# Counting neighbours with 32-column products, four in one PSUM bank, two tiles at a time

## The chip, the core and the metric

The kernel runs on one core of a Trainium2 chip. The metric is the device time in microseconds (us) of one launch; less is better.

## What is computed

Four layers of a graph network over N = 3327 nodes with D = 64 features share one dense-stored, sparse adjacency matrix `adj`. Each layer normalises, applies relu, and adds its result to `x`. All layers multiply by `adj`; together that makes eight hops. The one that matters here is layer 1, whose hop does not use the values of `adj` but the rank of each neighbour in its row:

```python
mask = (adj != 0).astype(support.dtype)
rank = jnp.cumsum(mask, axis=1)
deg = rank[:, -1:]
k = jnp.minimum(deg, 100.0)
pos = rank - (deg - k)
w = mask * jnp.where(pos > 0, 0.5 ** (k - pos), 0.0)
out = w @ support + bias
```

So for each row the number of nonzeros that lie behind a given column is needed: a count over whole blocks of 128 columns, and a count inside the block. The other layers are two gated cells (`adj @ (h W)`, then sigmoid and tanh gates), three products with `adj*adj`, and two products followed by tanh.

## The kernel before

The host hands over `adj` transposed and padded to 3328 = 26 x 128 in both directions. A *tile* is one block q of 128 source nodes (on the 128 partitions) against the targets of one *group*; there are 26 tiles per group and hop. The targets are folded: node n and node n + 1664 stand side by side (index s = 0, 1), so that a product of 128 rows and 64 columns for s = 0 and another for s = 1 fill the two column halves of TensorE and write the two halves of one PSUM bank. The target blocks are cut into four chunks: chunks 0 and 1 (384 columns each) form group 0, chunks 2 and 3 (384 and 512) form group 1.

The hops run in stages: `alone(0, 0)` does hop 0 of group 0; `joint(1, 0)` hops 0 and 1 of group 1 on one reading of the tiles; `joint(0, 1)` hops 1 and 2 of group 0, and so on. Each stage reads its group's tiles again, through a ring of 20 slots (`slots`, the list `dead` holds the free ones); loads are issued on SP in program order (L405), as soon as a slot is free. A hop is two products of a tile for each chunk (L678).

The order on every engine is written out by `run()`, unit by unit (hop, chunk, tile). Work around the hops is written as generators; a `yield us` in one puts it off until hops of about that many microseconds have been issued (`spend`). So the program order follows estimates, and the engines wait for one another where these are wrong. The nonlinear step behind a hop is such a task: the gates of a cell are L988 (128 rows by 64 columns) and L998 (64 rows by 64 columns).

The whole-block counts are units of their own (COUNT). For a tile q, a table `behind` supplies 64 columns of weights, such that output row r of the product counts the nonzeros of tile q if q lies behind block r. Summed over all 26 tiles this yields, for each block and target, the nonzeros behind it. It is made in two ways:

- Group 0, during `alone(0, 0)` (object `Counting`, after every tile): DVE writes the mask of the tile as f16 ones, 128x768, in two pieces (L498); TensorE takes four products of 64 columns and 384 streamed columns (L579), a pair for each chunk, each chunk into its own bank. At the end ACT copies the two banks into `totals` (L625).
- Group 1, during `joint(1, 0)` (object `Paced`, 0.55 tiles for each hop unit between unit 18 and 63, the rest at the end): the masks of s = 0 and s = 1 are packed into one number, 2047 for the first plus 1 for the second (L490, L493), so that a tile takes only one pair of products of 448 streamed columns (L592). At the end the sums are taken apart on DVE (`packed_done`, L606 to L609), sorted by two pairs of products with a table `sel` (L615), and copied by ACT (L616).

The `totals` are read by small DMAs on POOL (L504) into the last row of the masks of hop 2, and by `last_sources`. A mask takes half of a slot (`Mask`), a packed one a quarter (`Packed`).

Of the kernel before, what the change touches and what calls it, by code (L numbers as in the profile page):

```python
# [8 lines left out]

F32 = mybir.dt.float32  # L10
BF16 = mybir.dt.bfloat16
F16 = mybir.dt.float16
I16 = mybir.dt.int16
AF = mybir.ActivationFunctionType
ALU = mybir.AluOpType
# [31 lines left out]
P = 128  # L47
# [10 lines left out]
GWM = 7 * P  # L58
EPS = 1e-5
TWO7 = float(2 ** 7)  # L60
ROUND = float(3 * 2 ** 22)
DIGIT = 2047.0
LATE = 38
PACKED = 1
TWO27 = float(2 ** 27)
CAP = 100.0
BITS = (CAP - 128.0) * TWO7
# [34 lines left out]
def kernel(  # L102
# [35 lines left out]
    ident = const.tile([P, P], F32, name="ident")  # L138
    make_identity(nc, ident)
    tri = const.tile([P, P], BF16, name="tri")  # L140
    behind = const.tile([P, LATE + NQ - 1 + D], F16, name="behind")
    sel = const.tile([P, 2, D], F16, name="sel")
    bitsb = const.tile([P, 1], F32, name="bitsb")
    totals = [const.tile([P, sum(CH[c][1] - CH[c][0] for c in g) * P], BF16, name=f"totals{i}")
              for i, g in enumerate(GROUPS)]
# [4 lines left out]


    nc.gpsimd.memset(behind, 0.0)
    nc.gpsimd.memset(behind[:, LATE:LATE + NQ], 1.0)
    own = behind[:, LATE + NQ - 1:LATE + NQ]
    nc.gpsimd.affine_select(out=own, in_=own, pattern=[[0, 1]],
                            compare_op=ALU.is_gt, fill=0.0, base=2 - P, channel_multiplier=1)

# [77 lines left out]
    def more_constants():  # L235
# [15 lines left out]
        nc.gpsimd.memset(tri[:, P - 1:P], 0.0)  # L251
        nc.gpsimd.memset(bitsb, BITS)
        nc.gpsimd.memset(lasty, 0.0)
        nc.gpsimd.memset(sel, 0.0)
        wide = work.tile([P, P], F32, name="t2")
        nc.gpsimd.memset(wide, 0.0)

        for h in range(2):
            nc.vector.tensor_tensor(sel[:, h, :NQ], ident[:, h * D:h * D + NQ],
                                    ident[:, h * D + LATE:h * D + LATE + NQ], ALU.add)  # L260
        for i, (bi, bh) in enumerate(((BI1, BH1), (BI2, BH2))):
            nc.vector.tensor_add(bsum[:, i], bcol[:, bi:bi + 2], bcol[:, bh:bh + 2])

# [35 lines left out]
    def width(c):  # L299
        return blocks(c) * P  # L300
# [115 lines left out]

    spare = deque()

    quarters = deque()

    class Packed:

        def __init__(self, w):
            if not quarters:
                i = dead.popleft()
                quarters.extend((i, n) for n in range(4))
            self.at = quarters.popleft()
            i, n = self.at
            self.ones = slots[i].bitcast(F16).rearrange("p s w -> p (s w)")[:, n * GWM:n * GWM + w]

        def free(self):
            quarters.append(self.at)
            mine = [a for a in quarters if a[0] == self.at[0]]
            if len(mine) == 4:
                for a in mine:
                    quarters.remove(a)
                dead.append(self.at[0])

    class Mask:

        def __init__(self, w):
            if not spare:
                i = dead.popleft()
                spare.extend([(i, 0), (i, 1)])
            self.at = spare.popleft()
            i, h = self.at
            both = slots[i].bitcast(F16).rearrange("p s w -> p (s w)")
            self.ones = both[:, h * 2 * GWM:h * 2 * GWM + 2 * w].rearrange("p (s w) -> p s w", s=2)
            both = slots[i].bitcast(BF16).rearrange("p s w -> p (s w)")
            self.view = both[:, h * 2 * GWM:h * 2 * GWM + 2 * w].rearrange("p (s w) -> p s w", s=2)  # L450

# [29 lines left out]

    def make_mask(t, kind):

        t.mask = Packed(t.w) if kind == COUNT and t.g == PACKED else Mask(t.w)
        rows = P - 1 if kind == RANKED else P

        def piece(half):
            if kind == COUNT and t.g == PACKED:
                if half == 0:
                    nc.vector.tensor_scalar(t.mask.ones, t.view()[:, 0], 0.0, DIGIT,  # L490
                                            op0=ALU.not_equal, op1=ALU.mult)
                else:
                    nc.vector.scalar_tensor_tensor(t.mask.ones, t.view()[:, 1], 0.0, t.mask.ones,  # L493
                                                   op0=ALU.not_equal, op1=ALU.add)
                    t.used()
                return
            to = t.mask.ones if kind == COUNT else t.mask.view
            nc.vector.tensor_scalar(to[:rows, half], t.view()[:rows, half], 0.0, None, op0=ALU.not_equal)  # L498
            if half == 0 and kind == RANKED:

                for ch in GROUPS[t.g]:
                    finish(("count", ch))
                finish(("count", -t.g))
                nc.gpsimd.dma_start(out=t.mask.view[P - 1:P], in_=totals[t.g][t.q:t.q + D + 1:D, :])  # L504
            if half == 1:
                t.used()

        pieces.extend([(t, 0, piece), (t, 1, piece)])
# [57 lines left out]
    def count(t, first, last):  # L566


        mask_pieces(t=t)
        if t.g == PACKED:  # L570
            count_packed(t, first, last)
            return
        for c in GROUPS[t.g]:
            w = width(c)
            if first:
                counts[c] = take(either=False)
            at = LATE + NQ - 1 - t.q
            for s in range(2):
                nc.tensor.matmul(counts[c][1][s * D:(s + 1) * D, :w], behind[:, at:at + D],  # L579
                                 t.mask.ones[:, s, t.cols(c)], start=first, stop=last)  # L580
            spend(STREAM_US * w / CWM * 0.25)
            if last:
                begin(("count", c), count_done(c))
        t.mask.free()

    def count_packed(t, first, last):
        w = t.w // 2
        if first:
            counts[-t.g] = take(either=False)
        at = NQ - 1 - t.q + (LATE if t.q < NB else 0)  # L590
        for h in range(2):
            nc.tensor.matmul(counts[-t.g][1][upper(h), :w], behind[:, at:at + D], t.mask.ones[:, h * w:(h + 1) * w],  # L592
                             start=first, stop=last)
        spend(STREAM_US * t.w / CWM * 0.125)
        if last:
            begin(("count", -t.g), packed_done(t.g))
        t.mask.free()

    def packed_done(g):

        w = sum(width(c) for c in GROUPS[g]) // 2
        i, ps = counts.pop(-g)
        yield 30.0
        t = work.tile([P, CWM], F32, name="t2")[:, :w]
        n = work.tile([P, 2, CWM], F16, name="t2")[:, :, :w]
        nc.vector.tensor_scalar(t, ps[:, :w], 1.0 / DIGIT, -0.40625, op0=ALU.mult, op1=ALU.add)  # L606
        nc.vector.tensor_scalar(t, t, ROUND, None, op0=ALU.add)
        nc.vector.tensor_scalar(n[:, 0], t, ROUND, None, op0=ALU.subtract)
        nc.vector.scalar_tensor_tensor(n[:, 1], n[:, 0], -DIGIT, ps[:, :w], op0=ALU.mult, op1=ALU.add)  # L609
        give(i)  # L610
        yield 3.2
        for h in range(2):
            i, ps = take()
            for s in range(2):
                nc.tensor.matmul(ps[upper(s), :w], sel[:, h], n[:, s], start=True, stop=True)  # L615
            nc.scalar.copy(totals[g][:, h * w:(h + 1) * w], ps[:, :w])  # L616
            give(i)

    def count_done(c):
        g = c // 2  # L620
        w = width(c)
        w0 = (CH[c][0] - CH[GROUPS[g][0]][0]) * P
        i, ps = counts.pop(c)
        yield 0.48
        nc.scalar.copy(totals[g][:, w0:w0 + w], ps[:, :w])  # L625
        give(i)

    def last_sources(g):

        w = sum(width(c) for c in GROUPS[g])  # L630
        w0 = CH[GROUPS[g][0]][0] * P
        room = Mask(w)
        v = room.view.rearrange("p s w -> p (s w)").bitcast(F32)
        nc.gpsimd.memset(v, 0.0)
        yield 5.2
        rows = adjT.rearrange("(q p) (s n) -> q p s n", p=P, s=2)
        for s in range(2):
            nc.sync.dma_start(out=v[s * D:s * D + NQ], in_=rows[:, P - 1, s, w0:w0 + w])
        yield 48.0
        nc.vector.tensor_scalar(v, v, 0.0, 129.0 * TWO7, op0=ALU.not_equal, op1=ALU.mult)  # L640
        for c in GROUPS[g]:
            finish(("count", c))
        finish(("count", -g))
        yield 1.0
        nc.vector.scalar_tensor_tensor(v, totals[g], -TWO7, v, op0=ALU.mult, op1=ALU.add)
        yield 1.5
        nc.scalar.activation(lastw[g], v, AF.Relu, bias=bitsb)
        room.free()
# [44 lines left out]
    class Paced:  # L693
# [5 lines left out]
        def tick(self):  # L699
            self.n += 1  # L700
            if self.first <= self.n < self.last:
                self.due += self.rate
            while self.waiting and self.due >= 1.0:
                self.due -= 1.0
                t = self.waiting.popleft()
                put(COUNT, t.g, t)

        def rest(self):
            while self.waiting:
# [3 lines left out]
    class Counting:  # L713
# [3 lines left out]

        def add(self, t):
            self.waiting.append(t)
            if len(self.waiting) > self.lag:  # L720
                self.next()

        def next(self):
            put(COUNT, self.g, self.waiting.popleft())
# [480 lines left out]
```

## Time and profile before

| | us |
|---|---|
| median of three runs (683.25 to 683.5) | 683.35 |
| the profiled execution, its own time | 683.28 |
| its span, first to last instruction | 681.6 |

The granted TensorE clock of the profiled execution is 0.999. The first tile of group 0 is counted at about 10 us, the last at 62; group 1's counts run from 80 to 159 us.

In the lines of the profile, PE is the matrix product, PEld its weight load, DVE, ACT and POOL the other engines, SP the queue that issues loads. A matrix product in f32 is recorded as two passes, each with its own weight load. "128*64" behind an operation is the part of the array that it uses, rows by columns; two such on different halves run at once. Durations of products contain the time until the last result has left the array, so neighbouring ones overlap.

### The profile page before, as it was taken

What the parts mean: (1) busy time and instruction counts of PE and PEld (TensorE: products, weight loads), DVE (VectorE), ACT (ScalarE), POOL (GpSimd) and SP (SyncE); (2) the same over time, 40 slices, a digit from 0 to 9 for tenths busy, and PEclk for the clock granted to TensorE, in tenths of its full rate; (3) what the DMA queues carried; (4) which work ended last, traced back from release to release, by engine and by line L of the source; (5) the groups of instructions that cost most, each with busy time, mean ns of one, the idle gap of its engine ahead of it and who ended that gap; (6) DMA issues with size and microseconds to landing.
All of it is one profiled execution on the core that took longest, in us unless ns stands there. A gap on an engine that the chain in (4) does not pass through costs nothing.

```text
span 681.6 us, 12505 instructions
## 1 busy us (share of the span) xinstructions
PE 669.4 (98%) x4984; PEld 354.5 (52%) x4984; DVE 389.7 (57%) x839; ACT 270.5 (40%) x423; POOL 76.6 (11%) x115
## 2 busy tenths in 40 slices
PE   7999999999999999999999999999999999999997
PEld 5773444334556886566455554444444443344464
DVE  7954898749988999666552109225483893005101
ACT  1004000312248979999987009522366510000101
POOL 5400000002660503111000000000010000000000
PEclk9999999999999999999999999999999999999999
DMA  9999998399889615874999389954997399918991
GB/s 341 401 401 405 405 405 313 105 339 398 264 275 335 244 56 164 297 286 138 359 396 327 109 306 406 405 209 159 400 367 247 131 408 405 404 42 306 403 403 51
DMA packets 68693, 201.30 MB, mean 295 GB/s; under 512 B 7244, under 2 KB 8372, under 8 KB 68636
## 3 DMA queue, kind: packets, MB, share of 16 engines
q1 hardware_dynamic: 65724, 199.08, 78.3%
q10 hardware_dynamic: 736, 1.23, 0.5%
q8 instruction: 39, 0.64, 0.4%
q0 software_dynamic: 2176, 0.20, 0.2%
q14 instruction: 18, 0.15, 0.1%
HBM read 199.45 MB, written 0.85 MB: 294 GB/s over the span
## 4 chain that ended last, share of the span: by engine, by line
PE 91%; DVE 3%; DMA 3%; POOL 2%; issue 0%; ACT 0%; DVEq 0%; ACTq 0%; POOLq 0%
PE sum L678 79%; PE temp L307 5%; DMA adj<-in_adjT 2%; PE sum L307 2%; PE temp L988 1%; PE temp L867 1%; PE temp L592 1%; PE temp L579 1%; POOL both L239 1%; PE sum L988 1%; PE temp L998 1%; DVE e L554 0%; DMA xs<-in_x 0%; POOL st L947 0%; DVE adj L498 0%
## 5 line engine op out<-in xcount | busy, mean ns | idle before, releaser
L678 PE MATMUL sum<-adj,y 128*64 128x384 f32 (+3 forms) x3016 | 530.0, 501 | 1.1 <-DVE y L951 0.7
L678 PEld LDWEIGHTS sum<-adj,y 128*64 128x64 f32 x3016 | 235.4, 137 | 249.7 <-issue 167.2
L462 ACT ACTIVATE adj<-adj 128x768 f32<-128x768 f32 (+1 forms) x169 | 138.0, 890 | 26.9 <-DMA adj<-in_adjT 14.6
L498 DVE TENSOR_SCALAR adj<-adj 128x768 f16<-128x768 f32 (+2 forms) x156 | 85.3, 589 | 9.3 <-DMA adj<-in_adjT 7.3
L678 PE MATMUL sum<-e,both 128*64 128x384 bf16 (+1 forms) x624 | 72.6, 339 | 0.0
L923 ACT COPY both<-sum 64x384 f32<-64x384 f32 (+3 forms) x17 | 8.1, 478 | 161.7 <-PE sum L678 161.6
L556 ACT ACTIVATE e<-temp,bitsb 128x384 int16<-128x384 f32 (+1 forms) x112 | 63.0, 605 | 12.7 <-PE temp L307 11.3
L464 DVE TENSOR_TENSOR adj<-adj 128x768 f32<-128x768 f32 (+1 forms) x39 | 37.7, 1015 | 43.6 <-DMA adj<-in_adjT 32.4
L927 DVE COPY both<-sum 64x384 f32<-64x384 f32 (+3 forms) x11 | 6.2, 561 | 96.9 <-ACT both L923 95.7
L918 DVE STREAM_TRANSPOSE y<-t 32x96 f32<-32x96 f32 (+1 forms) x128 | 35.6, 278 | 40.4 <-ACT t L903 38.7
L947 POOL TENSOR_TENSOR st<-st,mhalf 128x6 f32<-128x6 f32 (+1 forms) x16 | 25.0, 1560 | 296.8 <-DVE st L945 296.8
L504 POOL DMA_DIRECT2D adj<-totals x52 | 31.7, 611 | 166.0 <-PE sum L678 128.8
L678 PEld LDWEIGHTS <-both 128*64 128x64 bf16 x624 | 42.8, 110 | 14.5 <-issue 3.6
L307 PE MATMUL temp<-adj,tri 128*64 128x384 bf16 (+1 forms) x314 | 47.1, 341 | 0.1
L554 DVE TENSOR_SCALAR e<-temp 128x384 int16<-128x384 f32 (+1 forms) x45 | 27.8, 619 | 18.7 <-ACT e L556 12.2
L896 DVE STREAM_TRANSPOSE both<-y 32x96 f32<-32x96 f32 (+1 forms) x128 | 35.6, 278 | 2.5
L307 PEld LDWEIGHTS <-tri 128*64 128x64 bf16 x416 | 28.7, 110 | 14.7 <-issue 8.6
L493 DVE SCALAR_TENSOR_TENSOR adj<-adj,adj 128x896 f16<-128x896 f32 x26 | 28.4, 1092 | 0.9
L903 ACT ACTIVATE t<-sum,hopcol 128x384 f32<-128x384 f32 (+1 forms) x8 | 4.9, 608 | 51.4 <-PE sum L678 48.5
L556 ACT ACTIVATE e<-sum,bitsb 128x384 int16<-128x384 f32 (+1 forms) x36 | 21.0, 593 | 5.0 <-PE sum L307 3.8
L579 PE MATMUL temp<-adj,behind 128*64 128x384 f16 x104 | 17.0, 327 | 2.1 <-DVE adj L498 1.9
L307 PE MATMUL sum<-adj,tri 128*64 128x384 bf16 (+1 forms) x102 | 17.6, 335 | 0.8 <-DVE e L554 0.5
(150 smaller groups left out, 345.3 us busy)
## 6 DMA issues: line engine op xcount, KB each, us to landing
adj<-in_adjT SPq DMA_DIRECT2D x130, 768.0 KB, 8.8
adj<-in_adjT SPq DMA_DIRECT2D x104, 896.0 KB, 13.4
xs<-in_x ACTq DMA_DIRECT2D x1, 448.0 KB
adj<-totals POOLq DMA_DIRECT2D x26, 3.0 KB, 4.9
adj<-totals POOLq DMA_DIRECT2D x26, 3.5 KB, 3.0
out<-xs ACTq DMA_DIRECT2D x1, 256.0 KB
xs<-in_x ACTq DMA_DIRECT2D x1, 192.0 KB, 3.2
xs<-in_x SPq DMA_DIRECT2D x1, 192.0 KB
```

The source lines that it names most:

```text
L307: nc.tensor.matmul(out[hs], lhsT[:, hs], rhs, start=start, stop=stop)
L462: nc.scalar.activation(sq, v, AF.Square)
L464: nc.vector.tensor_tensor(sq, v, v, ALU.mult)
L493: nc.vector.scalar_tensor_tensor(t.mask.ones, t.view()[:, 1], 0.0, t.mask.ones, op0=ALU.not_equal, op1=ALU.add)
L498: nc.vector.tensor_scalar(to[:rows, half], t.view()[:rows, half], 0.0, None, op0=ALU.not_equal)
L504: nc.gpsimd.dma_start(out=t.mask.view[P - 1:P], in_=totals[t.g][t.q:t.q + D + 1:D, :])
L554: nc.vector.tensor_scalar(wide[:, s], ps[:, :w], BITS, 0.0, op0=ALU.add, op1=ALU.max)
L556: nc.scalar.activation(wide[:, s], ps[:, :w], AF.Relu, bias=bitsb)
L678: nc.tensor.matmul(acc[h][1][h * D:(h + 1) * D, :w], yq[h], rhs[h], start=first and n == 0, stop=last and n == len(terms) - 1)
L896: nc.vector.transpose(to[at:at + 32, :, q], h[q * 32:(q + 1) * 32, :, s, f * 32:(f + 1) * 32])
L918: nc.vector.transpose(yk[q * 32:(q + 1) * 32, :, s, f * 32:(f + 1) * 32], v[at:at + 32, :, q])
L947: nc.gpsimd.tensor_tensor(st[:, 3, :n], st[:, 2, :n], mhalf[:, :n], ALU.pow)
```

## The change

All counts take one form. A product uses 32 columns of the array, and four of them, (s = 0, 1) x (two chunks), stand side by side in the four quarters of one PSUM bank. Both groups use it, each with ordinary two-piece masks, now bf16; the packed masks, their table `sel` and `packed_done` are gone. COUNT units are issued for two tiles at once (`BATCH`). At the end ACT puts the four quarters into their places in `totals` with four copies (group 0) or five (group 1), where the first ones also fill the rows between, which are not used.

```diff
-LATE = 38
-PACKED = 1
+ROWS = 32
+BATCH = 2
...
-    behind = const.tile([P, LATE + NQ - 1 + D], F16, name="behind")
-    sel = const.tile([P, 2, D], F16, name="sel")
+    behind = const.tile([P, NQ - 1 + ROWS], BF16, name="behind")
...
-        nc.gpsimd.memset(sel, 0.0)
...
-        for h in range(2):
-            nc.vector.tensor_tensor(sel[:, h, :NQ], ident[:, h * D:h * D + NQ],
-                                    ident[:, h * D + LATE:h * D + LATE + NQ], ALU.add)
...
-        t.mask = Packed(t.w) if kind == COUNT and t.g == PACKED else Mask(t.w)
+        t.mask = Mask(t.w)
...
-            to = t.mask.ones if kind == COUNT else t.mask.view
-            nc.vector.tensor_scalar(to[:rows, half], t.view()[:rows, half], 0.0, None, op0=ALU.not_equal)
+            nc.vector.tensor_scalar(t.mask.view[:rows, half], t.view()[:rows, half], 0.0, None, op0=ALU.not_equal)
...
         mask_pieces(t=t)
-        if t.g == PACKED:
-            count_packed(t, first, last)
-            return
-        for c in GROUPS[t.g]:
-            w = width(c)
-            if first:
-                counts[c] = take(either=False)
-            at = LATE + NQ - 1 - t.q
+        if first:
+            counts[t.g] = take(either=False)
+        at = NQ - 1 - t.q
+        for n, c in enumerate(GROUPS[t.g]):
             for s in range(2):
-                nc.tensor.matmul(counts[c][1][s * D:(s + 1) * D, :w], behind[:, at:at + D],
-                                 t.mask.ones[:, s, t.cols(c)], start=first, stop=last)
-            spend(STREAM_US * w / CWM * 0.25)
-            if last:
-                begin(("count", c), count_done(c))
+                row = (2 * s + n) * ROWS
+                nc.tensor.matmul(counts[t.g][1][row:row + ROWS, :width(c)], behind[:, at:at + ROWS],
+                                 t.mask.view[:, s, t.cols(c)], start=first, stop=last)
+        spend(STREAM_US * width(GROUPS[t.g][1]) / CWM * 0.25)
+        if last:
+            begin(("count", t.g), count_done(t.g))
         t.mask.free()
...
+    def count_done(g):
+        i, ps = counts.pop(g)
+        a, b = (width(c) for c in GROUPS[g])
+        yield 0.8
+        nc.scalar.copy(totals[g][:, :a], ps[:, :a])
+        nc.scalar.copy(totals[g][:, a:2 * a], ps[:, :a])
+        if b > a:
+            nc.scalar.copy(totals[g][:, b:], ps[:, :a])
+        for s in range(2):
+            nc.scalar.copy(totals[g][s * D:s * D + ROWS, a:], ps[s * D + ROWS:(s + 1) * D, :b])
         give(i)
...
-            while self.waiting and self.due >= 1.0:
-                self.due -= 1.0
-                t = self.waiting.popleft()
-                put(COUNT, t.g, t)
+            while self.waiting and self.due >= BATCH:
+                self.due -= BATCH
+                for t in list(self.waiting)[:BATCH]:
+                    put(COUNT, t.g, self.waiting.popleft())
...
-            if len(self.waiting) > self.lag:
-                self.next()
+            if len(self.waiting) >= BATCH + self.lag:
+                for _ in range(BATCH):
+                    self.next()
```

In the program order of the new kernel a batch of eight count products stands after every second tile in the first stage, and the last batch of group 0 is split around the gates of chunk 0. In `joint(1, 0)` twelve batches stand between hops, and a thirteenth follows the last hop unit of that stage's counting, as the two rest tiles did before.

More of the change, by code (lines that the diff above doesn't have):

```diff
@@ L11 @@
 BF16 = mybir.dt.bfloat16
-F16 = mybir.dt.float16
 I16 = mybir.dt.int16
@@ L60 @@
 TWO7 = float(2 ** 7)
-ROUND = float(3 * 2 ** 22)
-DIGIT = 2047.0
-LATE = 38
-PACKED = 1
+ROWS = 32
+BATCH = 2
 TWO27 = float(2 ** 27)
@@ L152 @@
     nc.gpsimd.memset(behind, 0.0)
-    nc.gpsimd.memset(behind[:, LATE:LATE + NQ], 1.0)
-    own = behind[:, LATE + NQ - 1:LATE + NQ]
+    nc.gpsimd.memset(behind[:, 0:NQ], 1.0)
+    own = behind[:, NQ - 1:NQ]
     nc.gpsimd.affine_select(out=own, in_=own, pattern=[[0, 1]],
@@ L417 @@
     spare = deque()
[L419 to L437, printed above, removed]
     class Mask:
@@ L446, in __init__ @@
             i, h = self.at
-            both = slots[i].bitcast(F16).rearrange("p s w -> p (s w)")
-            self.ones = both[:, h * 2 * GWM:h * 2 * GWM + 2 * w].rearrange("p (s w) -> p s w", s=2)
             both = slots[i].bitcast(BF16).rearrange("p s w -> p (s w)")
@@ L482, in make_mask @@
     def make_mask(t, kind):
-        t.mask = Packed(t.w) if kind == COUNT and t.g == PACKED else Mask(t.w)
+        t.mask = Mask(t.w)
         rows = P - 1 if kind == RANKED else P
         def piece(half):
[L488 to L495, printed above, removed]
-                return
-            to = t.mask.ones if kind == COUNT else t.mask.view
-            nc.vector.tensor_scalar(to[:rows, half], t.view()[:rows, half], 0.0, None, op0=ALU.not_equal)
+            nc.vector.tensor_scalar(t.mask.view[:rows, half], t.view()[:rows, half], 0.0, None, op0=ALU.not_equal)
             if half == 0 and kind == RANKED:
-                for ch in GROUPS[t.g]:
-                    finish(("count", ch))
-                finish(("count", -t.g))
+                finish(("count", t.g))
                 nc.gpsimd.dma_start(out=t.mask.view[P - 1:P], in_=totals[t.g][t.q:t.q + D + 1:D, :])
@@ L569, in count @@
         mask_pieces(t=t)
-        if t.g == PACKED:
-            count_packed(t, first, last)
-            return
-        for c in GROUPS[t.g]:
-            w = width(c)
-            if first:
-                counts[c] = take(either=False)
-            at = LATE + NQ - 1 - t.q
-            for s in range(2):
-                nc.tensor.matmul(counts[c][1][s * D:(s + 1) * D, :w], behind[:, at:at + D],
-                                 t.mask.ones[:, s, t.cols(c)], start=first, stop=last)
-            spend(STREAM_US * w / CWM * 0.25)
-            if last:
-                begin(("count", c), count_done(c))
@@ L584, in count @@
-        t.mask.free()
[L586 to L625, printed above, removed]
+        if first:
+            counts[t.g] = take(either=False)
+        at = NQ - 1 - t.q
+        for n, c in enumerate(GROUPS[t.g]):
+            for s in range(2):
+                row = (2 * s + n) * ROWS
+                nc.tensor.matmul(counts[t.g][1][row:row + ROWS, :width(c)], behind[:, at:at + ROWS],
+                                 t.mask.view[:, s, t.cols(c)], start=first, stop=last)
@@ L640, in last_sources @@
         nc.vector.tensor_scalar(v, v, 0.0, 129.0 * TWO7, op0=ALU.not_equal, op1=ALU.mult)
-        for c in GROUPS[g]:
-            finish(("count", c))
-        finish(("count", -g))
+        finish(("count", g))
         yield 1.0
```

## The prediction

> **What bounds the kernel now.** I read the page first: engine shares, the slices, the chain that ended last.
>
> ```profile
> span 681.6 us, 12505 instructions
> PE 669.4 (98%) x4984; PEld 354.5 (52%) x4984; DVE 389.7 (57%) x839; ACT 270.5 (40%) x423; POOL 76.6 (11%) x115
> ...
> PE 91%; DVE 3%; DMA 3%; POOL 2%; issue 0%; ACT 0%; DVEq 0%; ACTq 0%; POOLq 0%
> ```
>
> TensorE is the bound over the whole span, so what counts is TensorE time, stage by stage. The change touches the counts, which stand in two stages. The lines grouped by source give their present price (two columns: busy time and mean of one; a pair on the two halves of the array runs at once):
>
> ```profile
> L579 PE MATMUL temp<-adj,behind 128*64 128x384 f16 x104 | 17.0, 327 | 2.1 <-DVE adj L498 1.9
> L592 PE MATMUL temp<-adj,behind 128*64 128x448 f16 x52 | 9.4, 353 | 0.1
> L493 DVE SCALAR_TENSOR_TENSOR adj<-adj,adj 128x896 f16<-128x896 f32 x26 | 28.4, 1092 | 0.9
> L490 DVE TENSOR_SCALAR adj<-adj 128x896 f16<-128x896 f32 x26 | 16.1, 620 | 0.3 <-DMA adj<-in_adjT 0.3
> L615 PE MATMUL temp<-t,sel 128*64 128x448 f16 x4 | 0.6, 352 | 0.0
> ```
>
> These durations contain the tail of each product. What one occupies is read from starts, in the chain in order of time (start, length, what):
>
> ```profile
> 26.09 1.29 PE sum L678 x8
> 27.70 1.29 PE sum L678 x8
> ...
> 43.38 14.65 DMA adj<-in_adjT
> 58.07 1.51 PE sum L678 x8
> ...
> 80.63 1.50 PE sum L678 x8
> 82.32 1.50 PE sum L678 x8
> ```
>
> At 26 us a tile of group 0 takes 27.70 - 26.09 = 1.61: 1.29 of hop and 0.325 of two count pairs, so 0.1625 per pair of 384 columns. At 80 us a tile of group 1 takes 1.69: 1.505 of hop and 0.187 of one packed pair of 448. Neither shows anything lost between hop and count. Scaled by columns, a 512 pair takes 0.215 (0.1625 x 512/384).
>
> The same lines show the stages' different limits. The first stage ends with a DMA: the last group 0 tile releases TensorE at 58.07. The windows confirm it (columns: window, length, PE, PEld, DVE, ACT, POOL busy, clock, DMA share, GB/s):
>
> ```profile
> 9.70:58.00 48.30, 45.78 (x368) 32.81 (x364) 36.23 (x79) 4.27 (x9) 14.04 (x21) 1.00 1.03 401
> 58.00:65.30 7.30, 7.23 (x50) 2.74 (x50) 2.21 (x4) 5.52 (x10) 0.00 (x0) 1.00 1.03 407
> 65.30:160.00 94.70, 94.64 (x608) 38.45 (x606) 73.64 (x127) 13.01 (x24) 1.00 (x2) 1.00 0.85 323
> ```
>
> Up to 58 us the DMA engines are full: a 786 kB tile at 401 GB/s arrives each 1.96 us, against 1.61 of TensorE. From 65 to 160 TensorE never stops, and the DMA has slack. So a saving in group 0's counts is hidden behind its loads, while every change in group 1's counts moves the end.
>
> One more row is needed, since the counts will use another shape of the array: 128 rows by 32 columns amid 128x64 neighbours. The trace has no 32-column product, but it has another change of shape, in the gates: L988 (128x64), L998 (64x64), L678 (128x64). From the timeline of weight loads and products:
>
> ```profile
> 63.72 0.14 PEld L988 LDWEIGHTS temp<-both,cells 128*64 128x64 f32 x2 [0.18 <-issue]
> 64.46 0.13 PEld L998 LDWEIGHTS sum<-both,cells 64*64 64x64 f32 x1 [0.60 <-issue]
> 64.84 0.48 PE L998 MATMUL sum<-both,cells 64*64 64x384 f32 x1
> 65.27 0.20 PEld L678 LDWEIGHTS sum<-adj,y 128*64 128x64 f32 x4 [0.60 <-issue]
> 65.75 0.14 PEld L678 LDWEIGHTS sum<-adj,y 128*64 128x64 f32 x2 [0.29 <-issue]
> ```
>
> Within one shape, weights are loaded a whole product ahead (each 0.32). At a change the load waits 0.60 and comes together with its product. The last L988 pair starts 0.32 after 63.72 and ends streaming at 64.36. The two passes of L998 stream 0.645. Counting back one 512 pass (0.43) from 65.75, L678 effectively begins at 65.32. So the way there and back costs 65.32 - 64.36 - 0.645 = 0.31. The same sums at 151 us give 0.31 and at 162 us 0.34.
>
> **The change part by part.**
>
> *Group 1's counts (on the path).* Before, two tiles take 2 x 0.187 = 0.374. After, each tile is four 32-column products, the longest of 512 columns: 0.431 for two if the four run side by side, plus one change of shape there and back per batch of two. There are 13 batches. Nothing in this trace prices that change for 32 columns. The lower bound is nothing (as between f32 and f16 products of one shape above); the upper is the dearest excursion, 0.34, with one more exposed weight load (0.11, row L579's loads): 0.45. I take 0.30, near the measured 0.31, because that row is also a finer tiling inserted into 128x64 work. Sum: 13 x (0.431 + 0.30 - 0.374) = +4.6. Ends: 13 x 0.057 = +0.7 and 13 x 0.507 = +6.6.
>
> Here the Trainium skill speaks on both sides. "TensorE: Matmul & The Clock Gate", Part 3, models packed products as one product's time plus about 4 ns for each further tile. By that alone two tiles cost 0.431 + 2 x 0.012, and the batches add 13 x 0.081 = +1.1 instead of +4.6, and the total below would be about +0.8. But "TensorEngine Tiling (Array Packing)", Key Properties, says that changing the tiling mode, not just the tile, drains the engine; it gives no price. The 0.31 and the load that waits 0.60 fit that rule, for a change of both rows and columns; no run here yet shows it for columns alone. I follow the row.
>
> *Group 0's counts (covered).* Before, two tiles take 0.65; after, 2 x 0.1625 + 0.30 = 0.625. Cover: the loads up to 58.07. Even were TensorE slower there, 26 x 1.29 of hops, 8.3 of counts and some 4.3 of transposes and weights from 9.7 on end at 55.8, against 59.36, where the last tile's hop ends. That is over 3 us of slack. Cost 0; without that cover it would still be only -0.3.
>
> *The tail of that stage (on the path).* The last batch is split around chunk 0's gates. Before, one pair (0.16) sits before L988 and one after L998. After, a four-fold product sits in each place: the first needs the whole excursion (0.16 + 0.30, of which some 0.2 lies in the wait for ACT's two evacuation copies, until 59.58), the second lengthens a change of shape already there by half a trip, 0.15. Together about +0.35; bounds 0 and +0.6.
>
> *The packed group's epilogue.* Four L615 products, two pairs of 0.187, go: -0.37 on TensorE, on the path near 198 us. Four DVE operations (2.1) go with them.
>
> *DVE.* The second mask piece falls from 1.09 (L493) to the 0.62 of L490: 26 x 0.47 = 12.3 less, with the epilogue and the table for it 14.8. On the path it is worth one wait: at 157.4 to 159.2 the last two packed masks are late, and TensorE's last count waits some 0.2. Elsewhere DVE lies behind TensorE: 24 masks at 1.66 each run a few us ahead of their counts. I count -0.2; bounds 0 and -0.5. Were the masks' cover gone, it would be DVE that gains, not loses.
>
> *ACT.* Four copies into the totals become nine of about 0.5. For group 0 they follow the gates' four sigmoids and go ahead of the tanh, where two stand now: +1.0 for chunk 0's tanh. Its result is transposed by TensorE at 71.33, and is ready at 69.72: 1.6 of slack. For group 1 they lie between chunk 3's last sigmoid and its tanh, where ACT idles 2.0 for DVE: 0.5 late, and that node chunk is used many us later. Cost 0; if it did show, about +0.5 once. Queued behind the copies are only these tanh operations; the readers of the totals are POOL's small DMAs, and the second group's copies now come some 38 us earlier than before.
>
> *SP, POOL, slots.* The task clock counts 3.5 us less count work, so tasks started by it move. On SP the second cell's weight load (L160, issued at 92.05, landed 5.9 later) moves behind two more adjacency loads, which waited for slots until about 101 before. With 3.7 to issue it lands near 112; its reader L170 ran at 115.5 and moves behind chunk 2's gates, to about 122. The hop weights (L283, L285 at 132) go behind three more loads, some 10 us; their reader L209 ran at 172. The two last-row loads (L638) shift alike, and a mask slot more is at times taken during 75 to 115, when the queue is full anyway. POOL loses a 0.63 memset, before a DMA-bound stretch. Cost 0, bounds -1 and +1.
>
> **Sum.** 4.6 + 0.35 - 0.37 - 0.2 = +4.4. The profiled execution took 683.28, its span 681.6 and 1.7 around it; the median is 683.35, 0.07 away. I predict 683.3 + 4.4 = 687.7.
>
> **The rivals.**
>
> 1. *The change of shape is free.* Columns alone change, and the loader may run ahead as within 128x64. For: f16 pairs slip between f32 ones at no cost. Against: the 0.60 waits at L998. Price up to 0.1 per excursion: 13 x 0.157 = +2.0, +0.1 for the tail, -0.57: 684.9; at 0 it is 0.7 - 0.57 = +0.1, 683.5. Not measurable when the price is below 0.1 or so.
> 2. *Four 16-bit streams do not run at full rate.* Never more than two do in this trace. If they ran two by two, a batch would take 0.86 instead of 0.431: 13 x 0.43 = +5.6 more, 693.3. Against: the skill's packed figures. This is also the case in which the change would not do what it says.
> 3. *Faster: the relieved DVE decides the ranked stage.* From 160 to 210 DVE is busy 46.3 of 50, and it makes the ranked masks; 2.1 us fewer there would let masks and ranked weights run ahead. It decides only if ranked waits on TensorE exceed the +4.4. At free shape (rival 1) it needs 1.5 us, at full price 5.9. Against: TensorE is busy 49.96 of those 50, and 109.16 of the 110 after. Even if all 0.9 were won at free shape: 682.6, which is "same"; with slot and task order up to 1 better, 681.6.
>
> **How the numbers follow.** A change of 0.2%, 1.4 us, is about what a measurement of this kernel can tell. Forecast (excursion 0.2 to 0.4, 686.3 to 689.2): 0.63. Rival 1: 0.18, half of it within 0.2%, half slower. Rival 2, or a price above 0.45: 0.11. Rival 3: 0.08, of which 0.06 end faster and 0.02 the same. So slower 0.63 + 0.09 + 0.11 = 0.83; same 0.09 + 0.02 = 0.11; faster 0.06. The range from 683.9 to 691.0 leaves out rival 3, the free end of rival 1, and the dearest part of rival 2.
>
> **What would show it.** Right: in the new trace a batch of two counts between hops takes about 0.73 for group 1, from the end of one hop's streaming to the next, with the weight load before it and the hop's load after it both waiting about 0.6; hop periods of 80 to 115 us longer by some 0.17 per counted tile; the last group 0 tile still at about 58.1; L493 and L615 gone with no shorter wait on TensorE. Wrong: weights of the 32-column products loaded during the hop before (rival 1); the second tile's products starting 0.43 after the first's (rival 2); TensorE's work from 160 to 320 shortened (rival 3).

## The result and the profile after

The new kernel takes 689.58 us (689.55 to 689.62, four runs) against 683.36 before: a ratio of 1.0092, 95% interval 1.008 to 1.0104. It is slower by 6.2 us: the sign was forecast and the time lies inside the range, but the rise is 1.8 more than the likeliest value. The span grew from 681.6 to 687.9; the granted clock is 0.999 in both, so the clock has no part in it.

From the page of the new kernel, with one of its groups by line (busy time, mean of one); here and in the fences below, lines between those shown are left out:

```profile
span 687.9 us, 12583 instructions
PE 673.9 (98%) x5032; PEld 337.9 (49%) x5032; DVE 374.0 (54%) x833; ACT 272.8 (40%) x428; POOL 77.5 (11%) x114
PE 88%; DVE 4%; DMA 3%; POOL 2%; ACT 2%; issue 1%; ACTq 0%; DVEq 0%; POOLq 0%
L534 PE MATMUL temp<-adj,behind 128*32 128x384 bf16 x208 | 16.8, 346 | 1.6 <-DVE adj L458 1.4
```

DVE did become 15.7 us lighter (374.0 for 389.7). TensorE's share of the chain fell from 91% to 88%: other engines ended some of its waits. That is the first sign of a cost that the prediction did not have.

A batch in group 1's stage, from the timeline of weight loads and products:

```profile
81.88 0.14 PEld L601 LDWEIGHTS sum<-adj,y 128*64 128x64 f32 x2 [0.29 <-issue]
82.62 0.12 PEld L534 LDWEIGHTS <-behind 128*32 128x32 bf16 x8 [0.60 <-issue]
82.63 0.62 PE L534 MATMUL temp<-adj,behind 128*32 128x384 bf16 x8
83.17 0.20 PEld L601 LDWEIGHTS sum<-adj,y 128*64 128x64 f32 x4 [0.42 <-issue]
83.17 3.23 PE L601 MATMUL sum<-adj,y 128*64 128x512 f32 x16
86.33 0.62 PE L534 MATMUL temp<-adj,behind 128*32 128x384 bf16 x8
86.88 2.58 PE L601 MATMUL sum<-adj,y 128*64 128x512 f32 x12
```

The mark of a change of shape is there: L534's weights wait 0.60 for the hop's product to end, and are loaded in the moment of their own product; the hop's weights behind it wait 0.42. From the start of one hop run to the next, 86.88 - 83.17 = 3.71. Its sixteen passes stream 3.01 (two tiles of 1.505). So a batch occupies 0.70: 0.431 of streaming and 0.27 of changing shape there and back. The prediction had 0.30. The four products of a tile stream side by side: two by two, two tiles of 512 columns would take 0.86, more than the whole 0.70.

The first stage ended where it did:

```profile
43.27 14.71 DMA adj<-in_adjT
58.02 1.51 PE sum L601 x8
```

Now the two waits that are new. First the end of the gates of chunks 0 and 1, from the timeline of all engines, before and after:

```profile
65.80 0.64 ACT L1007 ACTIVATE adj<-adj,bcol 128x384 f32<-128x384 f32 x1
72.25 0.56 DVE L1058 COPY y<-sum 128x384 f32<-128x384 f32 x1
```


```profile
65.17 0.47 ACT L545 CAST totals<-temp 128x384 bf16<-128x384 f32 x1
65.52 0.49 ACT L546 CAST totals<-temp 128x384 bf16<-128x384 f32 x1
66.05 0.95 ACT L550 CAST totals<-temp 32x384 bf16<-32x384 f32 x2
67.03 1.12 ACT L931 ACTIVATE adj<-adj,bcol 128x384 f32<-128x384 f32 x2
72.15 0.56 DVE L937 TENSOR_TENSOR adj<-adj 128x384 f32<-128x384 f32 x1
72.74 0.35 DVE L939 TENSOR_SCALAR both<-adj 64x384 f32<-64x384 f32 x1
73.02 0.54 DVE L982 COPY y<-temp 128x384 f32<-128x384 f32 x1
73.61 0.87 PE L601 MATMUL sum<-adj,y 128*64 128x384 f32 x4 [0.46 <-DVE y L982]
```

Four ACT copies stand ahead of the two tanh (L931), which begin at 67.03, against 65.80 before. TensorE's transposes are not late (71.43 against 71.33). But the copy of their result (L982) stands on DVE behind the other chunk's gate operations (L937, L939), which are late; before, the same copy (L1058) began at 72.25. TensorE waits 0.46 for it.

Then, in the gates of chunks 2 and 3:

```profile
127.28 0.49 PE L166 MATMUL temp<-stage,ident 128*64 128x192 f32 x4
127.89 0.72 DVE L169 COPY cells<-temp 64x192 f32<-64x192 f32 x2 [9.27 <-PE temp L166]
128.54 0.60 DVE L925 SCALAR_TENSOR_TENSOR adj<-temp,bcol,adj 128x384 f32<-128x384 f32 x1
136.00 0.75 DVE L925 SCALAR_TENSOR_TENSOR adj<-temp,bcol,adj 128x512 f32<-128x512 f32 x1
139.88 2.37 PE L601 MATMUL sum<-adj,y 128*64 128x384 f32 x12 [0.76 <-DVE y L898]
```

The second cell's weights (L166, L169) ran before chunk 2's gates before (L170 at 115.5, gates at 120.06). Now they run inside them: L925 waits behind L169 on DVE. Before, hops ran from 129.71 on without a break (the chain below); now they stop for chunk 2's nodes (L898).

The chain before has these points:

```profile
73.72 0.70 PE temp L867 x24
129.71 19.70 PE sum L678 x108
162.95 6.60 PE sum L678 x40
394.39 162.79 PE sum L678 x936
```

How far behind the new kernel is, at the same work in both chains: first hop of group 1 +0.1 (65.36 for 65.27); after the second transpose near 74 us +0.8; start of the next stage +5.8 (168.75 for 162.95); end of the ranked stages +6.2 (400.56 for 394.39), and nothing more after that. Of the 5.0 between the second and third points, 13 x (0.70 - 0.374) = 4.2 is the price of the batches. Most of the rest is the second wait, of which the stop at 139.88 is 0.76.

### The profile page after: what moved, and what is told of

It reads as the page before. It is cut to its first block, busy times and chain, and to the rows that moved or that the text cites. A ratio compares the mean times of both kernels' runs of the same rounds, so it can differ in the third digit from the quotient of the medians.

```text
span 687.9 us, 12583 instructions
## 1 busy us (share of the span) xinstructions
PE 673.9 (98%) x5032; PEld 337.9 (49%) x5032; DVE 374.0 (54%) x833; ACT 272.8 (40%) x428; POOL 77.5 (11%) x114
## 4 chain that ended last, share of the span: by engine, by line
PE 88%; DVE 4%; DMA 3%; POOL 2%; ACT 2%; issue 1%; ACTq 0%; DVEq 0%; POOLq 0%
PE sum L601 76%; PE temp L299 5%; DMA adj<-in_adjT 2%; PE temp L534 2%; PE sum L299 1%; PE temp L791 1%; PE temp L912 1%; PE sum L912 1%; POOL both L235 1%; DVE y L898 1%; PE temp L922 0%; DVE adj L935 0%; ACT adj L432 0%; ACT e L514 0%; DMA xs<-in_x 0%
## 5 line engine op out<-in xcount | busy, mean ns | idle before, releaser
L601 PEld LDWEIGHTS sum<-adj,y 128*64 128x64 f32 x3016 | 226.2, 137 | 266.4 <-issue 182.3
L458 DVE TENSOR_SCALAR adj<-adj 128x768 bf16<-128x768 f32 (+3 forms) x208 | 113.2, 596 | 24.7 <-PE temp L534 19.6
L514 ACT ACTIVATE e<-temp,bitsb 128x384 int16<-128x384 f32 (+1 forms) x115 | 64.9, 607 | 9.4 <-PE temp L299 6.8
L851 DVE COPY both<-sum 64x384 f32<-64x384 f32 (+3 forms) x11 | 6.2, 561 | 98.8 <-ACT both L847 97.6
L299 PE MATMUL temp<-adj,tri 128*64 128x384 bf16 (+1 forms) x318 | 45.1, 342 | 0.8 <-DVE e L512 0.6
L514 ACT ACTIVATE e<-sum,bitsb 128x384 int16<-128x384 f32 (+1 forms) x33 | 18.8, 592 | 8.6 <-PE sum L299 7.1
L534 PE MATMUL temp<-adj,behind 128*32 128x384 bf16 x208 | 16.8, 346 | 1.6 <-DVE adj L458 1.4
L299 PE MATMUL sum<-adj,tri 128*64 128x384 bf16 (+1 forms) x98 | 14.2, 334 | 0.0
L875 DVE SCALAR_TENSOR_TENSOR y<-t,st 128x384 f32<-128x384 f32 (+1 forms) x16 | 9.5, 591 | 8.1 <-POOL st L871 7.9
```

Source lines behind the costliest of these rows:

```text
L299: nc.tensor.matmul(out[hs], lhsT[:, hs], rhs, start=start, stop=stop)
L458: nc.vector.tensor_scalar(t.mask.view[:rows, half], t.view()[:rows, half], 0.0, None, op0=ALU.not_equal)
L514: nc.scalar.activation(wide[:, s], ps[:, :w], AF.Relu, bias=bitsb)
L534: nc.tensor.matmul(counts[t.g][1][row:row + ROWS, :width(c)], behind[:, at:at + ROWS], t.mask.view[:, s, t.cols(c)], start=first, stop=last)
L601: nc.tensor.matmul(acc[h][1][h * D:(h + 1) * D, :w], yq[h], rhs[h], start=first and n == 0, stop=last and n == len(terms) - 1)
```

## The experiments

Theory 1: a batch costs a change of shape, there and back, of 0.27. Theories 2 and 3: the two waits come from the copies ahead of the tanh, and from the task clock's shift. The rival to 1 is streaming (four 16-bit streams, more weight loads).

**The change of shape alone.** The kernel before, with a tiny product behind every second packed count of group 1, 13 in all; the control has 64 columns in place of 32.

```diff
             nc.tensor.matmul(counts[-t.g][1][upper(h), :w], behind[:, at:at + D], t.mask.ones[:, h * w:(h + 1) * w],
                              start=first, stop=last)
+        seen[0] += 1
+        if seen[0] % 2 == 0:
+            i, ps = take(either=False)
+            nc.tensor.matmul(ps[0:32, :16], behind[:, 0:32], t.mask.ones[:, 0:16], start=True, stop=True)
+            give(i)
```

> The kernel before, with one extra product of 32 columns and 16 streamed columns after every second packed count of group 1 (13 in all), into a bank of its own; nothing reads it. Theory 1, the change of shape costs about 0.27 there and back: 13 x (0.27 + 0.01) = +3.6, 687.0. Rival, 32 columns amid 64 cost nothing and the new kernel is slower because four 16-bit streams or extra weight loads are slow: +0.4 at most, 683.8.

> The control: the same 13 extra products with 64 columns, the shape of their neighbours. Both theories: 13 x 0.03 = +0.4, 683.8; not more than +1. If it costs as much as the 32-column one, it is the extra product and its weight load that cost, not the shape.

Measured: 32 columns 686.64, ratio 1.0051 (1.0037 to 1.0065); 64 columns 683.96, 1.0011 (1.0004 to 1.0017), against 683.23. The timelines, first with 32 columns, then with 64:

```profile
82.17 0.09 PEld L598 LDWEIGHTS <-behind 128*32 128x32 f16 x1 [0.49 <-issue]
82.17 0.18 PE L598 MATMUL temp<-adj,behind 128*32 128x16 f16 x1
82.28 0.20 PEld L684 LDWEIGHTS sum<-adj,y 128*64 128x64 f32 x4
82.29 1.72 PE L684 MATMUL sum<-adj,y 128*64 128x512 f32 x8
```

```profile
82.13 0.11 PEld L598 LDWEIGHTS <-behind 128*64 128x64 f16 x1 [0.21 <-issue]
82.14 0.38 PEld L684 LDWEIGHTS sum<-adj,y 128*64 128x64 f32 x4
82.32 0.17 PE L598 MATMUL temp<-adj,behind 128*64 128x16 f16 x1
82.32 1.72 PE L684 MATMUL sum<-adj,y 128*64 128x512 f32 x8
```

In its neighbours' shape the product's weights, and those of the hop behind it, are loaded under the running count, and product and hop start together. With 32 columns the weights wait, and the hop's come after them. The difference is 2.7 us for 13, 0.21 each. So columns alone make the change of shape, and it costs with almost nothing streamed. Against the kernel before, a 32-column product costs 3.4/13 = 0.26, close to the 0.27 of a batch. The control costs 0.06 each over the whole stage, though only 0.01 at the place shown: its extra product runs on one half of the array, and in its trace the first product of a hop and the others, which start together at 82.32, stand 0.20 apart ten us later (91.83 and 92.03). Why this costs 0.06 stayed open.

**The number of batches.**

```diff
-            while self.waiting and self.due >= BATCH:
-                self.due -= BATCH
-                for t in list(self.waiting)[:BATCH]:
+            while self.waiting and self.due >= 1:       # and 4
+                self.due -= 1
+                for t in list(self.waiting)[:1]:
```

> The new kernel with group 1's counts issued one tile at a time: 26 excursions in place of 13, the same streaming. Theory 1: +13 x 0.27 = +3.5 over the new kernel, 693.1. Rival, streaming is what costs: 689.6, unchanged.

> The new kernel with group 1's counts issued four tiles at a time: 6 batches of four and one of two, 7 excursions in place of 13. Theory 1: -6 x 0.27 = -1.6, 688.0, if the masks of four tiles are ready in time. Rival: 689.6. If it is slower than 689.6, TensorE waits in the batch for masks that DVE makes at 1.25 a tile.

Measured: 692.66 and 687.87; ratios to the kernel before 1.0138 (1.0125 to 1.0152) and 1.0068 (1.0056 to 1.0081). The hops' starts, first with one tile at a time, then with four:

```profile
81.32 1.73 PE L601 MATMUL sum<-adj,y 128*64 128x512 f32 x8
82.98 0.40 PE L534 MATMUL temp<-adj,behind 128*32 128x384 bf16 x4
83.31 1.72 PE L601 MATMUL sum<-adj,y 128*64 128x512 f32 x8
```

```profile
86.45 5.59 PE L601 MATMUL sum<-adj,y 128*64 128x512 f32 x28
91.97 1.05 PE L534 MATMUL temp<-adj,behind 128*32 128x384 bf16 x16
92.95 4.30 PE L601 MATMUL sum<-adj,y 128*64 128x384 f32 x22
```

In these a lone tile occupies 0.48 (from 81.32 to 83.31, less 1.505 of hop), two 0.70, four 1.12 (86.45 to 92.95, less 5.375 of hop: four units of 0.86 and three of 0.645). That is 0.215 per tile plus 0.27 per batch, in all three. The rival, streaming, fails: with the streaming unchanged the time moved by +3.1 and -1.7 against the 689.58 of the new kernel.

**The copies and the task clock.** `late_copies` puts group 0's copies off, `old_clock` charges a count as before, `late_and_clock` does both.

```diff
-        yield 0.8
+        yield 14.0 if g == 0 else 0.8
         nc.scalar.copy(totals[g][:, :a], ps[:, :a])
```

```diff
-        spend(STREAM_US * width(GROUPS[t.g][1]) / CWM * 0.25)
+        spend(STREAM_US * t.w / CWM * (0.25, 0.125)[t.g])
```

> The new kernel with group 0's four copies into the totals put off until 14 us of hops later. Theory 2, these copies stand ahead of the tanh of chunk 0 and 1 on ACT and so make hop 1 wait at 73 us for chunk 0's nodes: -0.7, 688.9. Rival, that wait comes from the late end of the first stage: unchanged, 689.6.

> The new kernel with the task clock charged for a count as before the change, so that the tasks started by it (second cell's weights, hop weights, last rows) stand at their old places among the hops. Theory 3, their shift by 3.5 us of work put the second cell's weights and DVE's work on them into the gates of chunks 2 and 3, and lastw into the ranked squares: -0.8 at 139 us and -0.4 at 285 us, 688.4. Rival, these two waits come from other things: 689.6.

> Both together. Theories 2 and 3: 689.6 - 0.7 - 1.2 = 687.7, which would leave the 13 batches (13 x 0.33 = 4.2) as nearly all of the rest.

Measured: 688.84, 687.90 and 687.34, against 689.58. So the copies cost 0.7, the clock's shift 1.7, both 2.2. With both undone, the two waits are gone. The chains, new kernel first, then with both undone:

```profile
74.48 0.70 PE temp L791 x24
168.75 6.60 PE sum L601 x40
400.56 162.79 PE sum L601 x936
```

```profile
73.73 0.70 PE temp L791 x24
133.54 19.70 PE sum L601 x108
166.85 6.60 PE sum L601 x40
398.29 162.79 PE sum L601 x936
```

The second transpose stands at the time it had before (73.72), the hops from 133.54 run without a break, as before from 129.71, and the next stage and its end, at 166.85 and 398.29, are 3.9 behind the kernel before. What is left, 4.1 of time, is about what 13 batches cost (4.2). In `old_clock` the next stage starts at 167.67, 1.1 before the new kernel's 168.75, and the ranked stages end at 398.97, 1.6 before its 400.56. So 1.1 of the clock's shift is lost around the gates of chunks 2 and 3, and 0.5 in the ranked stages, where ACT makes the second group's last row (`lastw`, L570) at 286.5, and at 281.4 with the clock as before.

**Group 0 alone, and no counts in group 0.** In the first, group 1 stays packed, the clock is charged as before, and group 0 has the new form; in the second, the kernel before leaves out most of group 0's count products.

```diff
             for s in range(2):
-                nc.tensor.matmul(counts[c][1][s * D:(s + 1) * D, :w], behind[:, at:at + D],
-                                 t.mask.ones[:, s, t.cols(c)], start=first, stop=last)
+                if first or last:
+                    nc.tensor.matmul(counts[c][1][s * D:(s + 1) * D, :w], behind[:, at:at + D],
+                                     t.mask.ones[:, s, t.cols(c)], start=first, stop=last)
```

> Only group 0's counts in the new form (32 columns, two tiles at once), group 1's packed as before. The task clock is charged for group 0 as before. If the first stage's loads hide group 0's counts: the tail +0.1 and the copies' wait +0.7, so 684.2. Rival, the shape changes of the first stage show too: 13 x (0.60 + 0.27 - 0.65), 686 or more. A gain (the 4 us of halved streaming) would put it at 680.

> The kernel before without the count products of group 0's tiles 2 to 25 (their masks are still made; the counts are left out): 96 products, 48 x 0.1625 = 7.8 us of TensorE less in the first stage. If the loads bound that stage: unchanged, 683.4. Rival, TensorE bounds it: 675.6.

Measured: 683.69, 1.0007 (0.9999 to 1.0015), and 683.33, 1.0001 (0.9993 to 1.0009). Taking 7.8 us of TensorE work out of the first stage gains nothing: its loads hide group 0's counts wholly. The new form there costs 0.5 (interval -0.1 to 1.0), where 0.8 was expected of the tail and the copies. In its trace it is 0.9 behind near 74 us, as the new kernel is, and 0.5 from chunk 2's gates on (123.22 for 122.68). So most of the 6.2 is group 1's form, with the clock.

**A candidate: packed masks in 32 columns.** If side-by-side streams are at full rate, the packed form can use them too: tiles of the first and the second half of the sources go to different quarters. Products of 4, 6 or 8 tiles are held back and issued together; the counted tiles are reordered, so that halves alternate. A count is charged to the task clock at half its former cost.

```diff
+        held.append(t)
+        spend(STREAM_US * t.w / CWM * 0.0625)
+        if len(held) == 6 or last:                       # 4, 8
+            sides = [[u for u in held if u.q // NB == side] for side in range(2)]
...
+                            row = h * D + side * 32
+                            nc.tensor.matmul(counts[-t.g][1][row:row + 32, :w], behind[:, at:at + 32],
+                                             u.mask.ones[:, h * w:(h + 1) * w],
...
-        paced = Paced(others + all_own, *counted) if counted else None
+        paced = Paced([u for c in range(NC) for b in range(*CH[c]) for u in others + all_own if u.q % NB == b],
+                      *counted) if counted else None
```

> A candidate: the kernel before, group 1 packed as before, but its products of 32 columns: the tiles of the first and the second half of the sources go into different quarters of the bank, so two tiles stream at once; the products of six tiles are held back and issued together. A batch of six takes 3 x 0.187 + 0.27 = 0.83 in place of 1.12. Theory 1: 4 x -0.29 + 0.08 = -1.1, 682.3, unless the slots held by waiting masks delay loads. If four 16-bit streams ran at half rate: 4 x (1.39 - 1.12) = +1.1, 684.5.

> The same with eight tiles at once: 4 x 0.187 + 0.27 = 1.02 in place of 1.50, three times, and a last pair. Theory 1: -1.4 + 0.1 = -1.3, 682.0. At half rate +1, 684.4.

> The candidate with four packed tiles at once, whose masks fill just one slot. A batch takes 2 x 0.187 + 0.27 = 0.64 in place of 0.75, six times, and a last pair: -0.6 + 0.1 = -0.5, 682.7, if the loss of the six-tile form (TensorE waiting for a load at 113 us, for the last mask at 117 us, and in the later gates) came from slots and masks held. Rival, it comes from the new order of the counted tiles: +2 or more, 685.5.

Measured: 685.81, 685.89 and 685.59, ratios 1.0036 (1.0022 to 1.0049), 1.0041 (1.0028 to 1.0054) and 1.0035 (1.0021 to 1.0048). They miss what the theory of the change of shape gave by 2.9 to 3.9 us; the 685.5 that the last run's rival gave is met. The batches themselves do as planned: with six tiles the next hop starts 0.68 after the counts' start, where three sets stream 0.56, so two packed tiles share 0.187. The loss stands beside them. DVE and TensorE with four tiles:

```profile
116.00 0.63 DVE L490 TENSOR_SCALAR adj<-adj 128x896 f16<-128x896 f32 x1 [1.47 <-DMA adj<-in_adjT]
```

```profile
113.70 2.37 PE L691 MATMUL sum<-adj,y 128*64 128x384 f32 x12 [0.64 <-DMA adj<-in_adjT]
117.81 0.37 PE L603 MATMUL temp<-adj,behind 128*32 128x448 f16 x2 [1.25 <-DVE adj L493]
```

Masks wait for their tiles' loads, then TensorE for the masks: 0.64 and 1.25. The hops behind them are 1.4 late (131.09, and 129.64 in the timeline before); 0.8 more is lost by 202 us, and 0.4 between 278 and 291. Since four tiles fill one slot, and lose as much as six or eight, the held slots are not the main cause. Two differences are left. The new order of the counted tiles fits the two waits, as it asks for tiles before their loads have landed. The halved charge to the clock moves tasks, as in the new kernel: ACT makes the last row (`lastw`, L660) at 282.1, where the kernel before made it at 276.9, and the last 0.4 is lost around it. Neither was undone by itself, so the causes are argued and not shown. No version beat the kernel before.

## Why the prediction was right, and where its sizes were off

- *Group 1's batches*: the step held. Predicted 13 x 0.36 = +4.6, measured 13 x 0.33 = +4.2; the row of the gates (0.31) was a good guide to the price of the change (0.27). Batches of one, two and four tiles and the tiny products show it. The weights that wait 0.60 and 0.42 fit what the Trainium skill says under "TensorEngine Tiling (Array Packing)", Key Properties, that a change of mode drains the engine, now for columns alone. By the 4 ns for each further tile in "TensorE: Matmul & The Clock Gate", Part 3, alone the kernel would have stood at about 684, by the prediction's estimate, against the 689.58 measured.
- *Group 0's cover*: held, with the last load at 58.02 and 683.33 without its counts. The tail cost 0.1 and not 0.35.
- *DVE (-0.2)*: held. Before, the last two counts, from the transposes at 158.08 to the hop at 159.38, take 1.30. The products account for 0.70 and 0.374, so 0.23 is the wait for the last masks. With copies and clock undone, the same stretch (161.90 to 163.25) takes 1.35: 0.70 and a batch of 0.65, with no wait. So the 5.0 between the second and third points above is 4.2 for the batches and 1.1 for the second wait, less this 0.2 and a rest of 0.1.
- *ACT's copies, costed at 0*: a step that failed. "Its result is transposed by TensorE at 71.33, and is ready at 69.72: 1.6 of slack" followed only the first reader. The next link, DVE's copy of the transposed nodes, stood in order behind the other chunk's late gates and had no slack. It measured 0.7, where the prediction allowed 0.5 if it showed at all.
- *SP, POOL, slots, costed at 0 with bounds of 1*: a mis-sized term. The prediction followed the moved weight loads to their reader and found them in time, which they were. It did not ask into what the reader's own DVE work was moved: the gates of chunks 2 and 3 (1.1, most of it the wait at 139.88). About 0.5 more was lost in the ranked stages, where the last-row task stands later. Charging the clock as before gave 1.7 back, more than the bound of 1.
- *The packed epilogue (-0.37)*: L615 is gone, yet from 162.95 to 268.87 before and from 168.75 to 274.67 after the same work takes 105.92. At first the gain is there: the hop behind L615's place starts 5.4 behind (204.28 for 198.87), after 5.8. But the gates behind that hop wait for a copy on DVE (L851, 204.70 for 199.14), so that they end 5.6 behind. The last 0.2 is lost between 253 and 270; by what was not settled.
- *The rivals*: full-rate streams (rival 2 false), the change of shape not free (rival 1 false), ranked stage not faster (rival 3 false: it took 0.4 more).

So 4.4 + 2.2 (the two terms costed at 0) - 0.4 (cheaper batches) - 0.25 (tail) + 0.4 (epilogue) comes to 6.3, for the 6.2 measured. The sign and most of the rise follow from the mechanism that was forecast. That the time lies inside the range is in part luck: its width was meant for the price of the change of shape and for the rivals, and it took in 2.2 us of waits that the sum had left out.

## What to carry to other kernels

A product of another tile shape inside a stream of products paid here for the way there and back even with 16 columns; batch such products, or keep the shape, and read the price from the weight load that waits. When engines' order is written out by hand, an edit of an estimate moves work that has nothing to do with it: follow each moved task to every engine that it uses, and each delayed value through all of its readers in order, not to the first one only. A halved cost in a stage bound by loads is worth nothing, and the same cost in the next stage is worth all.

## What the runs showed of the hardware

- From 128x64 to 128x32 and back costs 0.27 with a batch in between; with one product of 16 columns it costs 0.21 more than the same product in 64 columns. A change of the columns alone suffices, and the next weights are not loaded ahead across it (waits of 0.60 and 0.42).
- Four 32-column products with 16-bit operands stream side by side at the rate of two of 64 columns: 0.215 for 512 columns, and 0.1625 for 384 before.
- A weight load of 32 columns took 93 ns (L534), one of 64 columns 110 (L579).
